# A two-layer graph network: the score stage with its products reordered, background work handed out per product, and VectorE in program order

## The chip, the cores and the metric

The kernel runs on one core of a Trainium2 chip. The core has a matrix engine (TensorE, PE in the profile; its weight loads are PEld), three engines for elementwise work (VectorE or DVE, ScalarE or ACT, GpSimd or POOL) and a queue that issues loads (SyncE, SP). PE writes only to PSUM, which has eight banks here; the others work between PSUM and SBUF, and DMA engines carry data between SBUF and the main memory (DRAM). The metric is the device time in microseconds (us).

## The reference

N = 2708 nodes, 1024 features, two layers, all in float32. `adj` is a 2708 x 2708 matrix of zeros and ones.

```python
def _L0_gnn_ref(x, adj, Wf, bf, Wg, bg, W, bW):
    f = x @ Wf + bf
    g = x @ Wg + bg
    e = jax.nn.relu(f @ g.T)
    scores = jnp.where(adj > 0, e, NEG)
    attention = jax.nn.softmax(scores, axis=1)
    return attention @ (x @ W + bW)

def _L1_gnn_ref(input, adj, W, a1, a2):
    h = input @ W
    e = jax.nn.leaky_relu(h @ a1 + (h @ a2).T, negative_slope=ALPHA)
    scores = jnp.where(adj > 0, e, neg)
    return jax.nn.relu(jax.nn.softmax(scores, axis=1) @ h)

h = jnp.maximum(_layernorm(x, axis=-1), 0.0)
x = x + _L0_gnn_ref(h, adj, ...)
h = jnp.maximum(_layernorm(x, axis=-1), 0.0)
x = x + _L1_gnn_ref(h, adj, ...)
```

## The kernel before

Every large matrix product is done as seven products of half the size (M1 to M7, the Strassen-Winograd scheme): both operands are split into quarters, sums of quarters are formed, the products are added up in PSUM and by VectorE.

The 2708 nodes are cut into five panels of columns (`panels`): two of 586 and three of 512. Each panel is cut into tiles of 128 rows, the last of a wide panel has 74; two tiles make a pair, and there are eleven pairs (`NQ` = 11). Layer 0 works on scores turned round: for a panel p, `scores(p, B)` (line 823) makes, for each pair q of rows, a block of 256 rows by the panel's columns. Its left sides are the normalized rows h, transposed, as seven sums of quarters; they were stored in DRAM as `hs_d[q]` in the order `BY_SCORES` and are loaded from there two at a time (`As`). Its right sides `B` come from `project_q(p)`, which multiplies h of the panel by the product of the weights.

Within a pair the seven products run in the order M1, M6, M5, M7, M2, M4, M3. X, Y and Z are three PSUM banks: M1 and M2 go to X, M5 and M3 to Y, M6, M7 and M4 to Z. After each product VectorE adds the bank to a tile: `sm1` (`sm` in the profile, two adds) from X, `st` from Z and from Y, then `Sb`, `Sa`, `Sb`, `Sa`. M7 adds to what M6 left in Z, so it may start only when VectorE has read Z; likewise M4 after M7, M3 after M5 and M2 after M1. All these adds go through the helper `add` (line 195); `sub` is line 198. Then the mask is added (line 880), the running maximum `acc` of a column is raised (line 885), and for rows that are `known` the maximum `mx` that layer 1 needs (`raise_max`, line 815).

Between these, `convert(q + 1)` makes the next pair's mask from `adj` on VectorE (lines 533 and 536), and `turn(q + 1)` transposes it on PE (line 546) and copies it on ScalarE (line 547).

Background work is kept in a list `later`, filled by `put(us, go, fetch, takes_psum)`. `behind(us)` adds us to a credit, at most twice us, and runs items while the credit is above zero; `one()` runs the next item and calls the `fetch` (a load) of the next two. `make_until(q)` forces items until the left sides of pair q are made. In the score stage `behind` is called once for a pair, with 4.0 in the first panel and 6.0 in the others. The items in the first panel are those of `make_pairs`: for rows that are not yet ready `norms` (layer norm: statistics on VectorE, a square root and a Relu on ScalarE), `rows` (sums of quarters stored to `hg_d`), `dots`, `transposes` (PE, copied by ScalarE to `hsT`) and `sums` (four VectorE sums, three stores from the GpSimd queue: two to `hs_d` and one of the quarter `a21` to `a21_d`). `hsT` is a pair of tiles with one buffer each, shared with `hT` and `gT`. In later panels the items are those of `rows_done` (line 934): for each finished row tile of layer 0 its layer norm, its two dot products, the sums of its pair and `put_max` for the panels already made.

The order in which each engine meets its instructions is fixed when the kernel is built: a scheduler places them by priority and by its own estimate of when operands are ready. Only the loads (`load`, line 98) are kept in program order on SP. Tiles come from pools: 54 slots, 12 stream buffers (`As`, `adj_i`, the sums `g`), and the eight banks.

Of the kernel before, what the change touches and what calls it, by code (L numbers as in the profile page):

```python
# [29 lines left out]
BY_SCORES = (M1, M6, M5, M7, M2, M4, M3)  # L30
# [3 lines left out]
def kernel(  # L34
# [19 lines left out]
    nc = tc.nc  # L54
# [53 lines left out]
    hs_d = [dram.tile([P, 7, NH, P], FP, name=f"hs_d{q}") for q in range(NQ)]  # L108
    a21_d = [dram.tile([P, NH, P], FP, name=f"a21_d{q}") for q in range(NQ)]
# [94 lines left out]
    def normalize(t):  # L204
# [8 lines left out]
        nc.scalar.activation(rs[:n, :1], mv[:n, 1:2], AF.Sqrt, bias=eps[:n])  # L213
        nc.vector.reciprocal(rs[:n, :1], rs[:n, :1])
# [27 lines left out]
    def make_pairs():  # L242
# [17 lines left out]
        def transposes(q):  # L260
            n = rows_of[q]
            lo, hi = (t[:, :4 * W].rearrange("p (m c j) -> p m c j", m=4, j=P) for t in both("hsT"))
            a21 = slot("a21", (P, NH, P))
            hT[q] = lo, hi, a21
            for k, e, o in ((0, 0, lo[:, 0]), (0, 1, hi[:, 0]), (1, 0, a21), (1, 1, hi[:, 1])):
                ps = bank("h_ps", (P, NH, P))
                for c in range(NH):
                    nc.tensor.transpose(ps[:, c, :n], xs[q][k][e][:, c * P:(c + 1) * P], ident[:n, :n])
                nc.scalar.copy(o[:, :, :n], ps[:, :, :n])

        def sums(q):
            n = rows_of[q]
            lo, hi, a21 = hT.pop(q)
            i = lambda t, k: t[:, k, :, :n]
            b = a21[:, :, :n]
            add(i(lo, 2), b, i(hi, 1))
            sub(i(lo, 1), i(lo, 2), i(lo, 0))
            sub(i(lo, 3), i(lo, 0), b)
            sub(i(hi, 2), i(hi, 0), i(lo, 1))
            if n == P:  # L280
                flat = lambda t, k: t[:, :k].rearrange("p m c j -> p (m c j)")
                nc.gpsimd.dma_start(hs_d[q][:, 0:4].rearrange("p m c j -> p (m c j)"), flat(lo, 4))
                nc.gpsimd.dma_start(hs_d[q][:, 4:7].rearrange("p m c j -> p (m c j)"), flat(hi, 3))
            else:
                nc.gpsimd.dma_start(hs_d[q][:, 0:4, :, :n].rearrange("p m c j -> p (m c) j"),
                                    lo[:, :, :, :n].rearrange("p m c j -> p (m c) j"))
                nc.gpsimd.dma_start(hs_d[q][:, 4:7, :, :n].rearrange("p m c j -> p (m c) j"),
                                    hi[:, :3, :, :n].rearrange("p m c j -> p (m c) j"))
            nc.gpsimd.dma_start(a21_d[q][:, :, :n], b)
# [145 lines left out]
    def project_q(p, then={}):  # L435
# [6 lines left out]
        for t, (_, n) in enumerate(panels[p], first[p]):  # L442
            q, k = pair_of[t]
            load(lo[:, :, o:o + n], hs_d[q][:, 0, :, :n] if k == 0 else a21_d[q][:, :, :n])
# [378 lines left out]
    def scores(p, B):  # L823
# [8 lines left out]
        S = [None] * NT  # L832
        for q in range(NQ):
# [6 lines left out]
            A = {}  # L840

            def product(m, ps, start):
                i = BY_SCORES.index(m)
                if i % 2 == 0:
                    A[i // 2] = stream("As", (P, 2, NH, P))
                    k = min(2, 7 - i)
                    if n == P:
                        load(A[i // 2][:, :k].rearrange("p m c j -> p (m c j)"),
                                          hs_d[q][:, i:i + k].rearrange("p m c j -> p (m c j)"))
                    else:  # L850
                        load(A[i // 2][:, :k, :, :n].rearrange("p m c j -> p (m c) j"),
                                          hs_d[q][:, i:i + k, :, :n].rearrange("p m c j -> p (m c) j"))
                for c in range(NH):
                    nc.tensor.matmul(ps[:n, :h], A[i // 2][:, i % 2, c, :n], B[m][c // 2][:, c % 2, :h],  # L854
                                     start=(start and c == 0), stop=(c == NH - 1), skip_group_check=True)

            X, Y, Z = (bank(f"s{k}") for k in "xyz")
            m1, t = slot("sm1"), slot("st")
            product(M1, X, True)
            for s in (lo, hi):  # L860
                add(m1[:n, s], X[:n, :h], rb[:n, s])
            product(M6, Z, True)
            add(t[:n, lo], Z[:n, :h], m1[:n, hi])
            product(M5, Y, True)
# [3 lines left out]
            product(M7, Z, False)  # L868
            add(sb[:n, hi], Z[:n, :h], t[:n, hi])
            product(M2, X, False)  # L870
            add(sa[:n, lo], X[:n, :h], rb[:n, lo])
            product(M4, Z, False)
            add(sb[:n, lo], Z[:n, :h], m1[:n, lo])
            product(M3, Y, False)
            add(sa[:n, hi], Y[:n, :h], t[:n, lo])
            if q + 1 < NQ:
                turn(q + 1)
            mk = mk_sb.pop((p, q))
            for k, s in enumerate((sa, sb)):
                nc.vector.scalar_tensor_tensor(s[:n, :w], s[:n, :w], 0.0, mk[:n, k, :w], op0=OP.max, op1=OP.add)  # L880
            for k, s in enumerate((sa, sb)):
                if q == 0 and k == 0:
                    nc.vector.tensor_copy(acc[:, :w], s[:, :w])
                else:
                    nc.vector.tensor_tensor(acc[:n, :w], acc[:n, :w], s[:n, :w], OP.max)
            if q in known:
                for k in range(2):
                    raise_max(p, q, k, mk[:n, k, :w])
            behind(4.0 if p == 0 else 6.0, True)
# [44 lines left out]
    def rows_done(t, xt):  # L934
# [4 lines left out]
        def dots():  # L939
            for k in range(2):  # L940
                dot(f[k][:n, t:t + 1], xt, [b[:n] for b in halves(wab[k])])
# [189 lines left out]
```

## Time and profile before

| | |
|---|---|
| times of three runs | 3283.95, 3287.55, 3278.29 us, median 3283.95 |
| the profiled execution | 3277.73 us, span 3276.0 us, mean granted TensorE clock 0.983 |
| HBM | read 535.23 MB, written 113.58 MB |
| `As<-hs_d` loads | 150 of 512 KB and 50 of 256 KB for whole pairs |
| stores of `hsT` to `hs_d` | 10 of 1024 KB (median 9.0 us to landing), 10 of 768 KB (10.5 us) |
| stores to `a21_d` | 10 of 256 KB (7.0 us) |

A line of instruction groups reads: line, engine, operation, output<-inputs by the program's names, shapes, how many | busy time in us, mean ns of one | idle time of the engine just before them, and what ended it. A line of the timeline reads: start, duration (both in us), engine, line, operation, tiles, how many in a row, and in brackets how long the engine had been idle before and what released it. A line of windows gives, for a stretch of the span, its length and each engine's busy time with the number of instructions, then the granted PE clock, the share in which the DMA engines were busy and GB/s. Matmuls of PE overlap: a product of eight matmuls listed at 1.89 or 2.14 us is followed by the next one 1.73 or 1.98 us after its start.

### The profile page before, as it was taken

To read this page: it belongs to the slowest core of one execution; us is meant where nothing else is said; L and a number is where in the kernel's file an instruction comes from. 1 tells how busy PE (TensorE), PEld (TensorE's weight loads), DVE (VectorE), ACT (ScalarE), POOL (GpSimd) and SP (SyncE) were. 2 spreads that over 40 slices of the span, in tenths; PEclk is the share of its full clock that TensorE was granted. 3 is DMA by queue.
4 is the path that set the end of the run, shared out by engine and by line. 5 is a ranking of instruction groups with operands and counts; after the bars stand their busy time and mean duration, and the time that the engine had idled before them with its cause. 6 is when DMAs were issued, how large, how long until landed. Compare 5 with 4: busy or idle time off the path is not lost.

```text
span 3276.0 us, 35270 instructions
## 1 busy us (share of the span) xinstructions
PE 3138.0 (96%) x12924; PEld 2331.6 (71%) x12924; DVE 1743.3 (53%) x3645; ACT 499.8 (15%) x833; POOL 331.4 (10%) x421
## 2 busy tenths in 40 slices
PE   8797899989999999999999999996999999999999
PEld 5375677747877478885788886873766748778585
DVE  6756577165551585616663257637665182553712
ACT  2312120010110110201020002103222030221300
POOL 1411102210001210012000101121010010000001
PEclk9998999999999999999999999998999999999999
DMA  5976848556645487456765566766555445565646
GB/s 216 361 249 246 295 150 323 172 184 209 188 136 156 133 265 222 143 185 196 232 194 149 155 205 208 237 210 238 172 170 174 149 144 182 180 194 176 195 149 212
DMA packets 284829, 651.17 MB, mean 199 GB/s; under 512 B 51919, under 2 KB 121539, under 8 KB 283377
## 3 DMA queue, kind: packets, MB, share of 16 engines
q1 hardware_dynamic: 252480, 535.31, 52.3%
q0 software_dynamic: 32176, 113.62, 9.0%
q8 instruction: 102, 1.67, 0.2%
q14 instruction: 71, 0.57, 0.0%
HBM read 535.23 MB, written 113.58 MB: 198 GB/s over the span
## 4 chain that ended last, share of the span: by engine, by line
PE 42%; issue 4%; DVE 4%; ACT 1%; DMA 0%; POOL 0%; SPq 0%; POOLq 0%; DVEq 0%; ACTq 0%
PE gz L416 8%; PE gy L416 8%; PE gx L416 8%; PE sz L854 3%; PE gv L416 3%; PE pz L752 3%; PE sx L854 2%; PE sy L854 2%; PE px L752 2%; PE py L752 2%; DVE sm L195 1%; DVE P L1053 1%; PE qz L416 1%; DVE P L195 1%; PE qy L416 0%
## 5 line engine op out<-in xcount | busy, mean ns | idle before, releaser
L854 PE MATMUL sz<-B,As 128*128 128x256 f32 (+3 forms) x1320 | 340.4, 402 | 43.9 <-DVE st L195 43.9
L854 PEld LDWEIGHTS sz<-B,As 128*128 128x128 f32 (+1 forms) x1320 | 249.6, 190 | 109.1 <-DVE st L195 49.8
L854 PE MATMUL sx<-B,As 128*128 128x256 f32 (+3 forms) x880 | 225.2, 398 | 9.9 <-DMA As<-hs_d 9.2
L854 PE MATMUL sy<-B,As 128*128 128x256 f32 (+3 forms) x880 | 218.9, 391 | 0.0
L416 PE MATMUL gy<-T,hc 128*128 128x256 f32 (+3 forms) x880 | 206.2, 396 | 5.4 <-DMA hc<-hg_d 3.0
L416 PE MATMUL gx<-P,hc 128*128 128x256 f32 (+3 forms) x880 | 204.5, 394 | 6.0 <-ACT P L1055 4.7
L416 PE MATMUL gz<-Sa,hc 128*128 128x256 f32 (+3 forms) x880 | 206.6, 393 | 0.0
L416 PE MATMUL gz<-P,hc 128*128 128x256 f32 (+3 forms) x880 | 206.3, 393 | 0.0
L687 POOL TENSOR_TENSOR gT<-gT,rr 128x2048 f32<-128x2048 f32 (+3 forms) x20 | 68.3, 3434 | 1316.0 <-DVE rr L134 519.8
L416 PEld LDWEIGHTS gx<-P,hc 128*128 128x128 f32 (+1 forms) x880 | 168.1, 191 | 42.5 <-ACT P L1055 5.0
L416 PEld LDWEIGHTS gy<-T,hc 128*128 128x128 f32 (+1 forms) x880 | 168.7, 192 | 41.4 <-DVE junk L172 3.4
L854 PEld LDWEIGHTS sx<-B,As 128*128 128x128 f32 (+1 forms) x880 | 161.2, 188 | 45.4 <-DVE r L173 9.4
L854 PEld LDWEIGHTS sy<-B,As 128*128 128x128 f32 (+1 forms) x880 | 163.0, 185 | 38.0
L416 PEld LDWEIGHTS gz<-Sa,hc 128*128 128x128 f32 (+1 forms) x880 | 165.5, 190 | 31.9
L416 PEld LDWEIGHTS gz<-P,hc 128*128 128x128 f32 (+1 forms) x880 | 165.5, 190 | 31.9
L547 ACT COPY mask<-mk_ps 128x1024 bf16<-128x1024 bf16 (+1 forms) x55 | 55.7, 1013 | 660.3 <-PE mk_ps L546 301.6
L752 PE MATMUL py<-w,ps 128*128 128x512 f32 (+1 forms) x352 | 155.5, 592 | 0.3 <-issue 0.3
L752 PE MATMUL px<-w,gT 128*128 128x512 f32 x320 | 144.8, 605 | 11.0 <-issue 9.6
L752 PE MATMUL pz<-w,ps 128*128 128x512 f32 (+1 forms) x352 | 155.0, 592 | 0.0
L752 PEld LDWEIGHTS pz<-w,ps 128*128 128x128 f32 (+1 forms) x352 | 65.4, 186 | 85.6 <-issue 82.5
L752 PEld LDWEIGHTS py<-w,ps 128*128 128x128 f32 (+1 forms) x352 | 65.4, 186 | 85.6 <-issue 83.2
L752 PEld LDWEIGHTS px<-w,gT 128*128 128x128 f32 x320 | 61.5, 194 | 87.2 <-issue 83.3
(240 smaller groups left out, 4721.9 us busy)
## 6 DMA issues: line engine op xcount, KB each, us to landing
hc<-hg_d SPq DMA_DIRECT2D x350, 512.0 KB
As<-hs_d SPq DMA_DIRECT2D x150, 512.0 KB
w<-wt_d SPq DMA_DIRECT2D x96, 512.0 KB
w<-in_L_gnn_W_dram SPq DMA_DIRECT2D x72, 512.0 KB
md<-md_d SPq DMA_DIRECT2D x70, 512.0 KB
adj_i<-in_adj_dram SPq DMA_DIRECT2D x50, 512.0 KB
hg_d<-g POOLq DMA_DIRECT2D x40, 512.0 KB, 5.9
As<-hs_d SPq DMA_DIRECT2D x50, 256.0 KB
```

Of the source, the lines that this page charges most:

```text
L195: nc.vector.tensor_tensor(o, a, b, OP.add)
L416: nc.tensor.matmul(ps[d], left(m, k, d), right(m, k), start=(start and k == 0), stop=(k == K - 1), skip_group_check=True)
L547: nc.scalar.copy(mk[:n, :, :k4 * P], ps[:n, :, :k4 * P])
L687: nc.gpsimd.tensor_tensor(of(e, s), of(e, s), by(s, k), OP.mult)
L752: nc.tensor.matmul(ps, left[i][m][:, k, :], w_[k], start=(start and k == 0), stop=(k == NH - 1), skip_group_check=True)
L854: nc.tensor.matmul(ps[:n, :h], A[i // 2][:, i % 2, c, :n], B[m][c // 2][:, c % 2, :h], start=(start and c == 0), stop=(c == NH - 1), skip_ ...
L1053: nc.vector.scalar_tensor_tensor(s, ub[:n, :w], f[1][:n, t:t + 1], s, op0=OP.add, op1=OP.max)
```

## The change

The order of products becomes M1, M6, M5, M2, M7, M3, M4, and a pair's M4 is issued after the next pair's M1 (`left_over`, `last`). Background work is handed out after each product: 0.6 in the first panel and 1.0 in the others, twice that after M3. From the first pair to the last of a score stage, every VectorE instruction is pinned behind the one traced before it on that engine (`InOrder`, `hold`). The mask, `acc` and `raise_max` of each half are done as soon as it is ready (`finish`). The layer norm of a row tile is split into `moments` and `normalize`, and the two dot products into two items. The quarter `a21` becomes an eighth block of `hs_d`, and the seven blocks stand there in the new order.

```diff
-BY_SCORES = (M1, M6, M5, M7, M2, M4, M3)
+BY_SCORES = (M1, M6, M5, M2, M7, M3, M4)
+class InOrder:
+    class Engine:
...
+        def __getattr__(self, name):
+            f = getattr(self.engine, name)
+            def issue(*a, **k):
+                i = f(*a, **k)
+                return self.owner.tc.keep_in_program_order(i) if self.owner.hold else i
+            return issue
...
-    nc = tc.nc
+    nc = InOrder(tc)
...
-    hs_d = [dram.tile([P, 7, NH, P], FP, name=f"hs_d{q}") for q in range(NQ)]
-    a21_d = [dram.tile([P, NH, P], FP, name=f"a21_d{q}") for q in range(NQ)]
+    hs_d = [dram.tile([P, 8, NH, P], FP, name=f"hs_d{q}") for q in range(NQ)]
...
         rs = stats.tile([P, 2], FP, name="rs")
         nc.scalar.activation(rs[:n, :1], mv[:n, 1:2], AF.Sqrt, bias=eps[:n])
+        of_rows[id(t)] = mv, rs
+    def normalize(t):
+        n = t[0].shape[0]
+        if id(t) not in of_rows:
+            moments(t)
+        mv, rs = of_rows.pop(id(t))
         nc.vector.reciprocal(rs[:n, :1], rs[:n, :1])
...
-            a21 = slot("a21", (P, NH, P))
-            hT[q] = lo, hi, a21
-            for k, e, o in ((0, 0, lo[:, 0]), (0, 1, hi[:, 0]), (1, 0, a21), (1, 1, hi[:, 1])):
+            hT[q] = lo, hi
+            for k, e, o in ((0, 0, lo[:, 0]), (0, 1, lo[:, 3]), (1, 0, hi[:, 3]), (1, 1, hi[:, 2])):
...
-            add(i(lo, 2), b, i(hi, 1))
+            add(i(lo, 2), i(hi, 3), i(hi, 2))
             sub(i(lo, 1), i(lo, 2), i(lo, 0))
-            sub(i(lo, 3), i(lo, 0), b)
-            sub(i(hi, 2), i(hi, 0), i(lo, 1))
+            sub(i(hi, 0), i(lo, 0), i(hi, 3))
+            sub(i(hi, 1), i(lo, 3), i(lo, 1))
...
-                nc.gpsimd.dma_start(hs_d[q][:, 4:7].rearrange("p m c j -> p (m c j)"), flat(hi, 3))
+                nc.gpsimd.dma_start(flat(hs_d[q][:, 4:8]), flat(hi))
...
-            nc.gpsimd.dma_start(a21_d[q][:, :, :n], b)
...
+        rate = 0.6 if p == 0 else 1.0
+        lefts = {}
...
+        def finish(q, s, k):
+            n, mk = rows_of[q], mk_sb[p, q]
+            nc.vector.scalar_tensor_tensor(s[:n, :w], s[:n, :w], 0.0, mk[:n, k, :w], op0=OP.max, op1=OP.add)
...
+                nc.vector.tensor_tensor(acc[:n, :w], acc[:n, :w], s[:n, :w], OP.max)
+            if q in known:
+                raise_max(p, q, k, mk[:n, k, :w])
+        def last(q, sb, Z, m1):
+            n = rows_of[q]
+            product(q, M4, Z, False)
+            add(sb[:n, lo], Z[:n, :h], m1[:n, lo])
+            finish(q, sb, 1)
+            mk_sb.pop((p, q))
+            behind(rate, True)
+        nc.hold = True
+        left_over = None
         for q in range(NQ):
...
-            product(M1, X, True)
+            product(q, M1, X, True)
             for s in (lo, hi):
                 add(m1[:n, s], X[:n, :h], rb[:n, s])
-            product(M6, Z, True)
+            if left_over:
+                left_over()
+            product(q, M6, Z, True)
             add(t[:n, lo], Z[:n, :h], m1[:n, hi])
-            product(M5, Y, True)
+            behind(rate, True)
+            product(q, M5, Y, True)
             add(t[:n, hi], Y[:n, :h], m1[:n, hi])
             if q + 1 < NQ:
                 convert(q + 1)
-            product(M7, Z, False)
+            behind(rate, True)
+            product(q, M2, X, False)
+            add(sa[:n, lo], X[:n, :h], rb[:n, lo])
+            behind(rate, True)
+            product(q, M7, Z, False)
             add(sb[:n, hi], Z[:n, :h], t[:n, hi])
...
+            behind(rate, True)
             if q + 1 < NQ:
                 turn(q + 1)
...
-            behind(4.0 if p == 0 else 6.0, True)
+            product(q, M3, Y, False)
+            add(sa[:n, hi], Y[:n, :h], t[:n, lo])
+            finish(q, sa, 0)
+            behind(2 * rate, True)
+            left_over = lambda q=q, sb=sb, Z=Z, m1=m1: last(q, sb, Z, m1)
+        left_over()
+        nc.hold = False
...
-        put(2.1, lambda: normalize(xt))
-        put(3.2, dots)
+        put(1.5, lambda: moments(xt))
+        put(0.5, lambda: normalize(xt))
+        put(1.6, lambda: dots(0))
+        put(1.6, lambda: dots(1))
```

## The prediction

> **What bounds the kernel now.** I read the busy times first, then the costliest groups with what ended the idle time before them, then busy times cut into the five score stages, and last the timelines of TensorE (PE), VectorE (DVE), ScalarE and the load queue (SP) around each gap.
>
> ```profile
> PE 3138.0 (96%) x12924; PEld 2331.6 (71%) x12924; DVE 1743.3 (53%) x3645; ACT 499.8 (15%) x833; POOL 331.4 (10%) x421
> ...
> L854 PE MATMUL sz<-B,As 128*128 128x256 f32 (+3 forms) x1320 | 340.4, 402 | 43.9 <-DVE st L195 43.9
> ...
> L854 PE MATMUL sx<-B,As 128*128 128x256 f32 (+3 forms) x880 | 225.2, 398 | 9.9 <-DMA As<-hs_d 9.2
> ```
>
> PE is the bound: only 138 us of the 3276.0 us span are not busy. 53.8 of these (43.9 + 9.9) stand before the score products of L854, which the change touches. Nearly all of them end with VectorE's `st`, one with a load of `As`.
>
> ```profile
> core 0: us, PE busy (x) PEld busy (x) DVE busy (x) ACT busy (x) POOL busy (x), PEclk, DMA share, GB/s
> 225.00:431.40 206.40, 179.95 (x831) 136.46 (x830) 116.59 (x229) 33.20 (x61) 22.98 (x41) 0.93 0.74 252
> 701.50:872.90 171.40, 160.81 (x720) 120.18 (x718) 95.63 (x193) 15.51 (x26) 11.62 (x20) 0.97 0.67 209
> 1149.00:1298.00 149.00, 140.89 (x698) 118.89 (x697) 100.70 (x216) 13.65 (x16) 16.99 (x24) 0.99 0.80 253
> 1530.60:1679.80 149.20, 140.53 (x698) 118.75 (x697) 98.99 (x204) 14.04 (x16) 14.10 (x20) 0.98 0.77 241
> 1864.30:2002.20 137.90, 137.90 (x698) 118.11 (x697) 79.18 (x155) 10.13 (x10) 17.81 (x18) 1.00 0.68 209
> ```
>
> The rows are the score stages P0 to P4, from first product to last. P4 has no gap at full clock: 137.9 is the floor for 256 columns, so P2 and P3 lie 11.1 and 11.3 above it. At 293 columns products start 1.98 apart and a pair's mask transposes take 0.53: 77 x 1.98 + 10 x 0.53 = 157.5, so P1 lies 13.9 above. P0 also holds seven sets of transposes of x at 1.77, floor 169.9: 36.5 above. Together **72.8 us**: 53.8 of idle PE and 19 of half clock after the gaps. That is all the change can win there.
>
> ```profile
> 255.58 4.27 PE L854 MATMUL sz<-B,As 128*128 128x293 f32 x8 [8.29 <-DVE st L195]
> ```
> ```profile
> 1573.02 5.84 DVE L815 SCALAR_TENSOR_TENSOR mx<-maskl,f,mx 128x586 f32<-128x586 bf16 x8
> ```
> ```profile
> 340.25 0.69 DVE L198 TENSOR_TENSOR hsT<-hsT,a 128x512 f32<-128x512 f32 x1 [8.41 <-ACT hsT L269]
> ```
> ```profile
> 339.63 0.59 ACT L269 COPY hsT<-h_ps 128x512 f32<-128x512 f32 x1 [10.46 <-DMA hs_d<-hsT]
> ```
> ```profile
> 267.36 13.86 SPq L98 DMA_DIRECT2D x<-in_x_dram  x4
> 281.31 0.39 SPq L98 DMA_DIRECT2D adj_i<-in_adj_dram  x1
> 281.79 0.31 SPq L98 DMA_DIRECT2D adj_t<-in_adj_dram  x1
> 282.15 1.77 SPq L98 DMA_DIRECT2D As<-hs_d  x4
> ```
>
> Three kinds of gap. First, order: M7 adds to the bank that held M6 and may start only when VectorE has read it, but VectorE had background work ahead of that add (rows, dots and norms of later rows at 241 to 254 and 706 to 715, a run of 5.84 us of `mx` at 1573). Second, a true wait: in P0 VectorE stood 8.41 us because ScalarE could not write `hsT` until the previous pair's store had landed. Third, SP: four loads of x waited for room and held the next pair's `As` back; PE then stood 9.23 us to 291.89.
>
> **The change, part by part.** *Reorder.* Products, matmuls and loads per pair are the same: 7, 56, 4. In before, one product (M5, 1.73 or 1.98 us) stands between M6 and M7, and one (M2) between M7 and M4. In after two stand everywhere (M5, M2; M3 and the next M1; M2, M7), and three between M1 and M2. VectorE may be late by 3.5 us (256 columns) or 4.0 (293) instead of 1.7 or 2.0. M4's `As` load moves behind the next pair's adjacency load and first `As` load on SP; it is needed a product after that first one, so it costs nothing while SP runs ahead. The last `Sb` of a stage comes an add, a max and an `acc` after the last product (0.42 + 2 x 0.69); `acc` is read only after 32 `qx` matmuls (6.9 us), which hide it.
>
> *Program order.* Every VectorE instruction of the stage stands where the code has it. This ends the first kind of gap. Behind a waiting instruction now stand all later adds, and PE waits for them once the 3.5 to 4.0 us are used up.
>
> *Background.* 7 x 0.6 = 4.2 us per pair instead of 4.0 in P0, 7.0 instead of 6.0 later, in pieces. Splitting normalize and dots adds no instruction; the Sqrt (0.29) falls between two handed-out pieces. VectorE's budget: P4 has 10.4 of `mx` in 79.2, so a pair needs (79.2 - 10.4)/11 = 6.3 without it. P2 has 18.4 on `x_res` and about 9 of loaded-mask `mx`: 27.4, spread by 7.0 over 3.9 pairs. In those VectorE has 27.4 + 3.9 x 7.3 (6.3 and about 1 of inline `mx`) = 55.9 against 3.9 x 12.59 = 49.1 of PE: 6.8 over, less 3.5 of grace, 3.3, plus about 2 for waits on ScalarE's Relu (rows of 0.55 to 1.25): **P2 keeps 5** of 11.1 (1 to 11). P3: 12.0 + 9.6 = 21.6 over 3.1 pairs, 44.9 against 39.0, likewise **4** of 11.3 (1 to 11). P1: 15 over 2.1 pairs at 7.4, 30.5 against 30.3: **1** of 13.9 (0 to 8, the start's backlog). P4: 0 (0 to 3). Without the grace P2 and P3 would keep 7 more. The pairs' `hg_d` stores on POOL and mask loads on SP move with the pieces; `hg_d` is read only in the aggregation, over 100 us later.
>
> *P0, by the same reckoning of credit.* (a) The gap of 8.29 and its slow product (4.07 instead of 1.98) go: 0 left. (b) The code still asks for pair 10's four x loads just ahead of pair 3's `As`, into a pool where one slot is freed (`a21`) and one `sm1` and a mask live longer. 9.23 and 2.9 of half clock stay, or go: 0 to 12; no row decides; **6**. (c) Pairs 6 to 10 of `hsT` follow through one buffer. From the last of its four sums to the next pair's last sum: issue 0.8, landing 10.8, copies 1.7, sums 2.8, about 16. The code puts them 8, 10, 12 and 14 us of PE work apart, so each is waited for; before, two such waits cost 6.45 and 2.48 with 3.9 of half clock, 12.8. Four waits of the longest seen, 8.4, less 4.0 grace, plus 2.1 clock each, would be 26; none if the spacing absorbs them. Nearest is before's row: **13**. (d) At pair 4 `rows`, `dots`, and pair 6's sums are forced in one piece: 2.8 + 3.4 + 2.8 = 9.0 ahead of `sm`; M2 comes due at 9.7 and `sm` at about 11.9, so 2.2 and 0.8 of clock: **3** (0 to 6). P0 keeps **22** of 36.5 (0 to 44).
>
> *One store instead of two.* 11 POOL issues of 0.55 us fewer, on an engine 10% busy; the second `hs_d` store grows from 768 to 1024 KB. By the rows of issue to landing (9.0 us for 1024 KB, 10.5 for 768 KB) that is -1.5 to +1.5 where the first projection waits for it; taken as 0.
>
> **Sum.** 72.8 - (22 + 1 + 5 + 4 + 0) = 41 us less. I allow 6 either way for later stages, whose schedule is laid anew, and take 39. The profiled execution took 3277.7 (span 3276.0 and 1.7 around it), which would become 3239; the median of the runs shown is 3283.95, so 3245.
>
> The Trainium skill, Perfetto Trace Analysis, Optimization Strategy, says that bubbles which recur can mean that SBUF or PSUM has no room for the next tile. That speaks against the change, since no reordering makes room. SP's wait on slots agrees at one place; by the rule alone (b) and (c) would stay whole and the sum be 35. TensorE: Matmul & The Clock Gate, What's actually happening, says that the clock halves after an idle window of about 3.4 us. The gap of 2.48 us at 362 was followed by a product of 3.76 instead of 1.98, so this trace shows it for less; by the rule the leftovers in P2 and P3 cost no clock.
>
> **Rivals.** *Only P1 to P3 heal*, P0 keeps 36.5: gain 72.8 - 36.5 - 10 = 26, time **3258**. For it: (b) and (c) are waits for room, not order. Against: the 8.29 gap is order. *Nearly all heals*: 8 left, **3219**. For it: P4 runs without a gap. Against: the 16 us chain. *Cancelled*: (b) 12, (c) 26, (d) 6 and two new waits on `hsT` at 6.5 make P0 57, with 18 kept in P1 to P3 75 against 72.8: **3286**, no change. *Slower*: VectorE's fixed order waits at its head. Place: the seven sums of P0 and the norms and dots of P1 to P3. Price: 7 x (8.4 - 4.0 + 2.1) + 3 + 12 = 60 in P0; 12 tiles at 2.3 (the longest wait of dots for Relu), the overloads 6.8 and 5.9 without grace, and six slow clocks of 2.1, 53, in P1 to P3. 113 against 72.8: **3324**. It decides once the held-up time passes 72.8; with P1 to P3 at 10, each of the seven waits would have to last 8.7. For it: the row of 8.41. Against: before's two sums were asked for back to back, after's are apart. That the order is not kept would be seen as hoisted work; it falls under the middle cases.
>
> **How the numbers follow.** Forecast 0.40, only P1 to P3 0.24, nearly all 0.10, cancelled 0.10, slower 0.16. A difference under 0.3%, 10 us, cannot be told from none. Faster: the first three, less 0.01, 0.73; same 0.10; slower 0.17. The forecast's own range is 3221 to 3266 (leftovers of 10 to 55). For 8 in 10 it goes from 3212 (5 left, and 4 less in later stages) to 3292 (P0 at 44, the others at their upper ends of 8, 11, 11 and 3, and 4 more in later stages).
>
> **What would show it.** VectorE: no background between M1's end and `sm` in P1; `mx` in ones and twos. PE: idle before L854 about 25 instead of 53.8; P1 near 159, P2 and P3 near 142, P0 near 192. Wrong if `hsT` waits grow beyond 8 us, if PE waits for `As` at more pairs, or if P4 leaves 137.9.

## The result, and the profile after

The changed kernel takes 3251.74 us (median of four runs, 3249.0 to 3252.34) beside 3282.73 for the kernel before (four runs): ratio 0.9904, 95% interval 0.9887 to 0.9921, 31 us less. The profiled execution took 3251.27 with a span of 3249.5, 26.5 less than the span of before. The profiled execution of before (3277.73) was quicker than its four timed runs, so the two traces show somewhat less than the medians.

The page's busy times and the score products, with the idle time before them in the last column:

```profile
PE 3136.1 (97%) x12924; PEld 2330.0 (72%) x12924; DVE 1753.1 (54%) x3648; ACT 499.9 (15%) x833; POOL 326.2 (10%) x410
...
L877 PE MATMUL sz<-B,As 128*128 128x256 f32 (+3 forms) x1320 | 327.5, 397 | 2.9 <-DVE st L44 2.9
...
L877 PE MATMUL sx<-B,As 128*128 128x256 f32 (+3 forms) x880 | 224.2, 398 | 13.0 <-DMA As<-hs_d 9.5
```

The 43.9 us in front of `sz` are down to 2.9, and what stands in front of `sx` is the load of `As`, as before. Looked at this way 38 us of PE's 53.8 idle before the score products are gone. But the stages, in busy times by window, do not give up 38:

```profile
221.60:413.00 191.40, 177.87 (x832) 134.78 (x830) 114.45 (x230) 33.80 (x61) 19.55 (x34) 0.96 0.78 271
681.00:845.00 164.00, 160.50 (x720) 120.08 (x718) 97.66 (x199) 15.80 (x27) 12.39 (x22) 0.99 0.68 218
1121.00:1268.50 147.50, 140.52 (x699) 118.80 (x698) 102.94 (x214) 13.76 (x16) 15.29 (x22) 0.99 0.77 252
1501.00:1648.20 147.20, 140.50 (x699) 119.03 (x698) 101.42 (x207) 14.34 (x17) 14.39 (x21) 0.99 0.75 245
1832.60:1975.40 142.80, 139.97 (x699) 119.34 (x698) 86.36 (x156) 10.13 (x10) 18.47 (x19) 0.99 0.62 198
```

| stage | before | after | above its floor | forecast above floor |
|---|---|---|---|---|
| P0 | 206.4 | 191.3 | 21.4 | 22 |
| P1 | 171.4 | 163.9 | 6.4 | 1 |
| P2 | 149.0 | 147.4 | 9.5 | 5 |
| P3 | 149.3 | 147.2 | 9.3 | 4 |
| P4 | 137.9 | 142.7 | 4.8 | 0 |

A stage's floor is the length that the prediction worked out for it without a gap (169.9, 157.5 and three times 137.9). The stages are 21.4 shorter in sum, where 41 were forecast: P0 by 15.1, P1 by 7.5, P2 and P3 by 1.6 and 2.1, and P4 is 4.8 longer. The first begins 3.4 earlier and the stretch between P0 and P1 is 2.1 shorter; the stretches between the later stages have the same length to 0.1 (276.1, 232.5, 184.5), and the tail is 0.4 longer.

**Where the idle time went.** Seen by tile, the mask transposes on PE (line 574) have a line of idle time that before did not have:

```profile
L574 PE MATMUL mk_ps<-identb,nm x440: 217/219/248, 212.6 to 1954.9; 128*128 128x128 bf16 x134, 128*74 128x128 bf16 x13
...
its engine sat idle before it (us, times) until:
  DVE nm L44: 15.2, 8
```

Eight times PE stood before the transposes until VectorE had made the next pair's mask (`nm`): twice in P1, three times each in P2 and P3. One of them, in the timeline of PE and VectorE:

```profile
1138.82 1.89 PE L877 MATMUL sx<-B,As 128*128 128x256 f32 x8
...
1140.32 0.42 DVE L44 TENSOR_TENSOR st<-sz,sm 128x256 f32<-128x256 f32 x1
...
1142.38 0.41 DVE L44 TENSOR_TENSOR st<-sy,sm 128x256 f32<-128x256 f32 x1
1142.71 0.46 DVE L44 TENSOR_SCALAR nm<-adj_i 128x592 bf16<-128x592 int32 x1
...
1143.22 0.64 PE L574 MATMUL mk_ps<-identb,nm 128*74 128x128 bf16 x8 [2.51 <-DVE nm L44]
1143.70 1.95 PE L877 MATMUL sz<-B,As 128*128 128x256 f32 x8
```

M7 (`sz`) was ready at 1140.74, when `st` had been read out of Z. It started at 1143.70, because on PE the transposes stand ahead of it. The code has them behind M7. Only VectorE is pinned: PE's order was still laid by the scheduler, and in these eight pairs it put the transposes between M2 and M7. That its estimate of when the mask is ready led it to do so is argued, not shown.

**P4** lost to something else. Around its one wait:

```profile
1957.29 7.37 POOL L1038 TENSOR_TENSOR x_res<-x_res,bwb 128x512 f32<-128x512 f32 x6
...
1957.49 7.72 DVE L44 SCALAR_TENSOR_TENSOR Sa<-Sa,mask 128x512 f32<-128x512 f32 x1
...
1966.66 0.70 PE L877 MATMUL sx<-B,As 128*128 128x256 f32 x2 [2.83 <-DVE sm L44]
```

One VectorE instruction that takes 0.69 us elsewhere took 7.72, beside six GpSimd adds of 7.37 together. Before, these adds ran from 1992.4, where VectorE had almost only additions that read PSUM, which no GpSimd instruction of these traces does.

**P0** has the waits that the prediction named under (b) and (c), in PE's timeline:

```profile
272.25 4.25 PE L877 MATMUL sx<-B,As 128*128 128x293 f32 x8 [5.64 <-DMA As<-hs_d]
...
294.41 3.34 PE L877 MATMUL sx<-B,As 128*128 128x293 f32 x8 [2.58 <-DMA As<-hs_d]
...
316.39 1.11 PE L299 MATMUL h_ps<-ident,x 128*128 128x128 f32 x4 [2.38 <-DVE Sa L44]
...
331.24 2.25 PE L877 MATMUL sz<-B,As 128*128 128x293 f32 x8 [2.92 <-DVE st L44]
```

### The profile page after: what moved, and what is told of

Same layout as the page of the kernel before. It is cut to its first block, busy times and chain, and to the rows that moved or that the text cites. A ratio compares the mean times of both kernels' runs of the same rounds, so it can differ in the third digit from the quotient of the medians.

```text
span 3249.5 us, 35289 instructions
## 1 busy us (share of the span) xinstructions
PE 3136.1 (97%) x12924; PEld 2330.0 (72%) x12924; DVE 1753.1 (54%) x3648; ACT 499.9 (15%) x833; POOL 326.2 (10%) x410
## 4 chain that ended last, share of the span: by engine, by line
PE 77%; issue 6%; DVE 4%; DMA 3%; POOL 1%; ACT 1%; POOLq 0%; SPq 0%; DVEq 0%; ACTq 0%
PE gz L444 12%; PE gy L444 12%; PE gx L444 12%; PE sz L877 7%; PE sy L877 5%; PE gv L444 5%; PE sx L877 5%; PE pz L780 4%; PE py L780 3%; PE px L780 3%; PE qz L444 3%; PE qy L444 2%; PE qx L444 2%; DMA hs_d<-hsT 1%; PE mk_ps L574 1%
## 5 line engine op out<-in xcount | busy, mean ns | idle before, releaser
L877 PE MATMUL sz<-B,As 128*128 128x256 f32 (+3 forms) x1320 | 327.5, 397 | 2.9 <-DVE st L44 2.9
L780 PE MATMUL px<-w,gT 128*128 128x512 f32 x320 | 145.1, 606 | 11.9 <-issue 10.4
```

Of the source, the lines that this page charges most:

```text
L780: nc.tensor.matmul(ps, left[i][m][:, k, :], w_[k], start=(start and k == 0), stop=(k == NH - 1), skip_group_check=True)
L877: nc.tensor.matmul(ps[:n, :h], lefts[q][:, i % 2, c, :n], B[m][c // 2][:, c % 2, :h], start=(start and c == 0), stop=(c == NH - 1), skip_g ...
```

## The experiments

All are edits of the changed kernel. Times are medians beside runs of the kernel before on the same chip (3280.6 to 3283.5 us); stage lengths are from one trace each.

| kernel | time | ratio to before, 95% | P0 | P1 | P2 | P3 | P4 |
|---|---|---|---|---|---|---|---|
| changed | 3251.7 | 0.9904 (0.9887 to 0.9921) | 191.3 | 163.9 | 147.4 | 147.2 | 142.7 |
| changed, again | 3253.4 | 0.9904 (0.9886 to 0.9921) | 192.9 | 163.9 | 148.0 | 147.2 | 142.7 |
| VectorE's order free | 3251.9 | 0.9901 (0.9888 to 0.9915) | 193.8 | 167.9 | 142.6 | 144.5 | 141.4 |
| background in one lump | 3279.4 | 0.9981 (0.9972 to 0.9990) | 188.2 | 168.5 | 161.8 | 157.6 | 141.4 |
| old order of products | 3279.2 | 0.9984 (0.9975 to 0.9993) | 193.1 | 169.4 | 154.6 | 157.9 | 139.8 |
| transposes later in the code | 3262.0 | 0.9931 (0.9918 to 0.9943) | 194.0 | 163.9 | 146.6 | 149.3 | 146.2 |
| late bias | 3257.4 | 0.9925 (0.9911 to 0.9940) | 193.2 | 163.8 | 147.2 | 149.0 | 137.9 |
| x fetched later | 3247.7 | 0.9901 (0.9885 to 0.9918) | 186.5 | 163.8 | 146.5 | 145.4 | 142.6 |
| 0.75 a product | 3246.0 | 0.9889 (0.9875 to 0.9904) | 190.8 | 162.5 | 140.5 | 149.1 | 142.7 |
| transposes pinned on PE | 3250.0 | 0.9901 (0.9884 to 0.9919) | 193.6 | 158.5 | 149.1 | 145.5 | 145.5 |
| pinned, x later, bias on VectorE | 3240.4 | 0.9872 (0.9856 to 0.9888) | 186.3 | 158.5 | 149.5 | 144.2 | 137.9 |
| the same with 0.75 | 3235.4 | 0.9853 (0.9836 to 0.9869) | 185.7 | 162.3 | 139.2 | 145.5 | 137.9 |
| the same, bias on GpSimd with gaps | 3230.1 | 0.9838 (0.9824 to 0.9853) | 187.0 | 160.6 | 138.5 | 144.9 | 137.9 |

**How far one trace can be trusted.** The changed kernel was run once more:

> The changed kernel once more, unaltered, on the chip of the next two: what two profiles of one kernel differ by. All theories: 3247-3256, stages of P1 to P4 within 1 of 163.9, 147.4, 147.2 and 142.7; P0 and the stretch between P0 and P1, which wait for DMAs, may differ by 2 to 4 us each; VectorE's instruction of 7.7 us in P4 is there again.

P1 to P4 came back within 0.6 us, with the same waits at the same pairs and the long VectorE instruction (7.73). P0 was 1.6 longer, and the stretch between P0 and P1 272.7 against 268.1. The span was 3255.3, 20.7 less than before's. So differences of 2 us in P0 or 5 in a whole span say nothing. In P1 to P4 a difference of 2 us is more than these two traces differ by, though not by much more than happens: the last two kernels of the table have the same code up to P4 and differ by 1.7 in P1.

**What does it: order, pieces or reorder?** Three kernels each take one part away.

```diff
-        nc.hold = True
```

> The changed kernel with VectorE's instructions no longer pinned: products reordered, background still in pieces, the order left to the scheduler. Theory 'order': the gain comes from background no longer standing ahead of the adds that a product waits for; without the pin the scheduler hoists it again, PE's idle time before the score products rises from 13 to 30 us or more and the time from 3252 to 3262-3277. Rival 'slack': the reorder alone gives VectorE two products of room, which covers whatever order the scheduler lays; then the time stays at 3248-3256 and the score stages at their lengths (191, 164, 147, 147, 143).

3251.9, the same time as with the pin: my theory that the pinned order brings the gain falls. The idle time before the score products shows what the pin gives and takes:

```profile
L877 PE MATMUL sz<-B,As 128*128 128x256 f32 (+3 forms) x1320 | 323.0, 393 | 8.5 <-DVE st L44 7.2
...
L877 PE MATMUL sx<-B,As 128*128 128x256 f32 (+3 forms) x880 | 224.1, 398 | 21.1 <-DVE sm L44 14.8
L877 PE MATMUL sy<-B,As 128*128 128x256 f32 (+3 forms) x880 | 223.9, 397 | 4.2 <-DVE st L44 4.2
```

Without the pin PE idles 8.5 + 21.1 + 4.2 = 33.8 us before the score products: background ran ahead of `sm` at the start of P1 (a wait of 6.80) and ahead of `st` in P0 (3.80 and 6.88). With it PE idles 2.9 + 13.0 there, 15.2 before the mask transposes and 2.4 before transposes of x, 33.5 (without it 0.5 before the two kinds of transposes). The pin ends one kind of wait and makes another of the same size.

```diff
-            behind(rate, True)
...
-            behind(2 * rate, True)
+            behind(7 * rate, True)
```

The five single calls go, the one behind M3 hands out all.

> The changed kernel with the same background credit (4.2 us a pair in the first stage, 7.0 later) handed out once, after M3, instead of in seven pieces; VectorE still in program order. Theory 'pieces matter': a lump of 7 us is 3.5 us more than the room that two products give, so about 3.5 us and a slow product of 2 are lost for each of the some 4 + 4 + 3 pairs with a full lump in the second to fourth stage, and a few in the first: 3275-3300. Rival 'room alone': the lump stands where Sa is done and the next M1 needs nothing, so that three products cover it: 3250-3258.

3279.4, as the theory had it. PE idles 47.5 us before `sx`, nearly all for `sm`, the first add behind the lump:

```profile
L877 PE MATMUL sx<-B,As 128*128 128x256 f32 (+3 forms) x880 | 235.8, 413 | 47.5 <-DVE sm L44 42.4
```

P2 and P3 are 14.4 and 10.4 longer than in the changed kernel and longer than before. P0, where a lump is 4.2 us, is not (188.2). The lump of 7.0 is also more than the 6.0 of the kernel before; the new order with 6.0 in one lump was not run.

```diff
-            product(q, M2, X, False)
-            add(sa[:n, lo], X[:n, :h], rb[:n, lo])
-            behind(rate, True)
             product(q, M7, Z, False)
             add(sb[:n, hi], Z[:n, :h], t[:n, hi])
             behind(rate, True)
+            product(q, M2, X, False)
+            add(sa[:n, lo], X[:n, :h], rb[:n, lo])
+            behind(rate, True)
             if q + 1 < NQ:
                 turn(q + 1)
+            last(q, sb, Z, m1)
             product(q, M3, Y, False)
...
-            left_over = lambda q=q, sb=sb, Z=Z, m1=m1: last(q, sb, Z, m1)
-        left_over()
```

> The changed kernel with the products in the order of before (M1, M6, M5, M7, M2, M4, M3, no product left over for the next pair); pieces of background after each product, VectorE in program order, one store of a pair's sums as in the changed kernel. Theory 'both are needed': VectorE may be late by one product (1.7 or 2.0 us) instead of two, and pieces of 1 to 2.7 us beside the two adds after M1 exceed that several times a stage: PE idle before the score products 25 to 45 us, time 3265-3290. Rival 'order of VectorE is enough': 3250-3258.

3279.2, again as the theory had it: in the old order the same pieces cost P2 7.2 and P3 10.7 us more, though of P2's idle time 3.97 us end with a load of masks and not with VectorE. So with one of the two parts taken away 4 us of the 31 are left in the whole time. In P2 and P3 two products of room are about as much as one piece needs and not enough for a lump; one product is not enough for a piece.

By stage this explains less than it seems. P0 fell from 206.4 to 191.3 and stays at 188.2 to 193.8 in all three kernels, so neither the pin, nor the pieces, nor the reorder is needed for the largest part of the gain by itself. What the three share besides (the sums stored with `a21` in two stores instead of three, a tile less, the mask added half by half, 4.2 us of background instead of 4.0) was not taken away, so the cause in P0 stays open. P1, 7.5 shorter, gives back 4.0 to 5.5 without any one of the three. P2 and P3 gained only 1.6 and 2.1; without the pieces or without the reorder both stages are longer than before, with 7.0 us of background a pair instead of 6.0.

**The wait before the mask transposes.** First the transposes were moved in the code alone:

```diff
-            if q + 1 < NQ:
-                turn(q + 1)
             product(q, M3, Y, False)
+            if q + 1 < NQ:
+                turn(q + 1)
```

> The changed kernel with the next pair's mask transposes placed behind M3 instead of ahead of it; nothing else. Theory 'new wait': what P1 to P3 kept (6 to 9 us each) is PE standing in order before these transposes until VectorE has made the next mask (3.5, 5.7 and 6.1 us by the trace); one product more of room ends most of it: P1 to P3 shorter by 10 to 15 us together, time 3237-3244. Rival 'overload': VectorE has more work than PE in those pairs and the wait only moves to sx, sy or sz: stages shorter by less than 3, time 3249-3254.

3262.0, slower than either theory said, and the eight waits are there at the same pairs (14.7 us instead of 15.2). One of them:

```profile
1146.53 1.89 PE L877 MATMUL sx<-B,As 128*128 128x256 f32 x8
1150.42 0.64 PE L574 MATMUL mk_ps<-identb,nm 128*74 128x128 bf16 x8 [2.00 <-DVE nm L44]
1150.90 1.95 PE L877 MATMUL sz<-B,As 128*128 128x256 f32 x8
```

The transposes still follow M2 and precede M7: in 32 of the 40 pairs of P1 to P4 they moved behind M3, in these eight the scheduler put them where it had before. So this run does not decide between the theories. Of the 10 us that it is slower P4 has 3.5 (a wait of 4.94 instead of 2.83 at the long instruction, which lasts 8.51 here). The rest is spread over P0, P3 and the stretch between P0 and P1; in P0 and that stretch it is about what the second trace of the changed kernel has too, and in P3 it is a wait for `sm` that is looked at below. The next kernel pins them:

```diff
-                    nc.tensor.transpose(ps[:n, k, i * P:(i + 1) * P], m[0][:, i, k, :n], identb)
+                    o = nc.tensor.transpose(ps[:n, k, i * P:(i + 1) * P], m[0][:, i, k, :n], identb)
+                    if nc.hold:
+                        tc.keep_in_program_order(o)
```

> The changed kernel with the mask transposes behind M3 in the code and each of them pinned behind the instruction traced before it on PE, so that they stand there on the chip too (in the changed kernel and with the transposes merely moved in the code, 8 of the 40 pairs of P1 to P4 have them ahead of M7, 2, 3 and 3 in P1, P2 and P3, as many as there are waits for nm). Theory 'PE's order': M7 was ready while PE stood before the transposes; the waits for nm fall from 15.3 to under 4 us, P1 to 159-162, P2 and P3 to 140-143, time 3237-3245. Rival 'overload': VectorE is behind by as much in sum, PE then waits before sz or sy for st, or before sx for sm; P1 to P3 shorter by less than 4 together, 3248-3255.

The waits for `nm` are gone, all 15.2 us. P1 fell by 5.4 to 158.5, one above its floor: there the theory holds. P2 rose by 1.7, P3 fell by 1.7, as the rival said: PE now waits for `st` (2.23 in P2, 0.49 to 0.77 in P3), for `sm` (1.97 at the start of P3) and, in P2, 4.00 us for `As`. P4 is 2.8 longer, where M7 takes a wait of 4.93 for the long instruction. The three stages together are 5.4 shorter, between what the theory and the rival said, and the time is the same within the interval. The stand before the transposes was a place, not the whole cause; the work that made VectorE late stayed.

**How much background a pair can take.**

```diff
-        rate = 0.6 if p == 0 else 1.0
+        rate = 0.6 if p == 0 else 0.75
```

> The changed kernel with 0.75 instead of 1.0 us of background after each product in the second to fifth stage, 5.25 instead of 7.0 a pair. Theory 'overload': with the 7.3 us that a pair needs of VectorE itself, 7.0 make 14.3 against 12.6 of PE, and the excess of some four pairs is what P2 and P3 kept; 5.25 make 12.55, so the waits before the mask transposes (5.7 and 6.1) go, P2 and P3 fall from 147 to 139-143, P1 by 0-5, time 3237-3244. Rival 'where a piece stands': pieces are as large as before (2.7, 1.5, 1.6 us) and still stand ahead of the next mask, in more pairs; P2 and P3 stay at 145 or more, time 3248-3254.

P2 fell to 140.5 as the theory said, 2.6 above its floor. P3 did not fall (149.1): its waits for `nm` are shorter, 3.8 us instead of 6.1, but PE waited 3.64 us for `sm` at the start. The time, 3246.0, lies between the two forecasts and is not told apart from the changed kernel's. The same wait stands in the last-but-one kernel of the table, where it is the only one left in P3:

```profile
1495.37 0.81 ACT L249 ACTIVATE x_res<-x_res,rs 128x512 f32<-128x512 f32 x1 [4.08 <-DMA x_d<-x_res]
1496.22 0.69 DVE L44 SCALAR_TENSOR_TENSOR junk<-x_res,wab 128x512 bf16<-128x512 f32 x1 [4.92 <-ACT x_res L249]
...
1497.77 0.74 DVE L44 TENSOR_TENSOR sm<-sx,rb 128x256 f32<-128x256 f32 x2
1498.57 1.65 PE L879 MATMUL sx<-B,As 128*128 128x256 f32 x3 [4.52 <-DVE sm L44]
```

ScalarE's Relu writes over `x_res` in place and waits until its store has landed; the dot product waits for the Relu; `sm` stands behind the dot product on VectorE; M2, which adds to X, waits for `sm`. This is the mechanism of the rival called *Slower*, a wait at VectorE's head, at one place. The wait for `sm` at the start of P3 is 0.6 us in both traces of the changed kernel and 0.6 to 4.5 in the others that have it; where it is longest (2.8 to 4.5), ScalarE waited 2.5 to 4.1 for that store. Handing the Relu another tile was not tried.

**P4.** First the adds were moved out of the stage:

```diff
-                    nc.gpsimd.tensor_add(xs[t][e], xs[t][e], bwb[e][:n, :W])
+                    if p != NP - 2:
+                        nc.gpsimd.tensor_add(xs[t][e], xs[t][e], bwb[e][:n, :W])
...
             add(xs[t][e], c, xs[t][e])
+            if p == NP - 2:
+                nc.gpsimd.tensor_add(xs[t][e], xs[t][e], bwb[e][:n, :W])
```

> The changed kernel with GpSimd's eight adds of the bias bwb to the residual rows of the fourth panel moved from where the rows are loaded (inside the last score stage) to behind VectorE's add in the projection that follows. Theory 'GpSimd holds VectorE up': the instruction Sa<-Sa,mask of 7.72 us lay beside six of these adds (7.37 us together); without them it takes 0.69, the wait of 2.83 us before sx and the slow product go, the fifth stage falls from 142.7 to 137.9-138.5 and the time by 4-5 us to 3246-3249. Rival 'something else held it' (the loads of these rows, or the mask): an instruction of VectorE beside the row loads is long again, the stage stays at 141 or more, time 3250-3254.

P4 is 137.9, its floor, without a wait: GpSimd's adds had held VectorE up. The time did not follow (3257.4): in the projection behind it PE waited 6.35 us for `pt` from VectorE instead of 2.72, and one of the moved adds took 4.06. The stretch behind the stage is 1276.4 us, against 1274.1 and 1272.5 in the two traces of the changed kernel, so 2.3 to 3.9 of the 4.8 went back there; why the median is higher still is not explained. The last kernel of all (otherwise the one with 0.75 under *Together*) leaves the adds in the stage but puts something between them that reads nothing:

```diff
-                    nc.gpsimd.tensor_add(xs[t][e], xs[t][e], bwb[e][:n, :W])
+                    i = nc.gpsimd.tensor_add(xs[t][e], xs[t][e], bwb[e][:n, :W])
+                    if p == NP - 2:
+                        tc.keep_in_program_order(i)
+                        for _ in range(4):
+                            tc.keep_in_program_order(nc.gpsimd.memset(gap, 0.0))
```

> The last one, but with the fourth panel's bias left on GpSimd and four small memsets (128 x 8) between one add and the next. It asks how VectorE came to stand for 7.7 us beside six adds of 1.2 us. Theory 'held add by add': GpSimd takes the shared way into SBUF again before VectorE can, back to back; with something between that reads no SBUF, VectorE's instruction gets in after one add, takes 0.7 to 2.5 us, and P4 is 137.9-139. Rival 'held as long as adds are queued, whatever lies between' or 'memsets hold it too': an instruction of 7 us or more, P4 142-147. The rest as in the run before, within 3 us.

```profile
1952.90 1.26 POOL L1041 TENSOR_TENSOR x_res<-x_res,bwb 128x512 f32<-128x512 f32 x1
1952.96 1.75 DVE L44 TENSOR_TENSOR acc<-acc,Sa 128x512 f32<-128x512 f32 x1
1954.10 0.59 POOL L1045 MEMSET gap<- 128x8 f32 x4
1954.63 0.41 DVE L44 TENSOR_TENSOR Sb<-sz,sm 128x256 f32<-128x256 f32 x1
1954.68 1.26 POOL L1041 TENSOR_TENSOR x_res<-x_res,bwb 128x512 f32<-128x512 f32 x1
1955.08 1.41 DVE L44 SCALAR_TENSOR_TENSOR Sb<-Sb,mask 128x512 f32<-128x512 f32 x1
```

VectorE's instructions with both operands in SBUF now wait for one add at most (1.75 and 1.41 instead of 0.69), the one that reads PSUM takes its usual 0.41, and P4 is at its floor. That is what the theory said. The adds are spread by the memsets too, so that fewer meet VectorE; both belong to the edit. And the memsets are not the only way in: in the kernel with the old order of products GpSimd's first four adds follow each other with nothing between, and VectorE takes turns with them.

```profile
1989.79 6.33 POOL L1039 TENSOR_TENSOR x_res<-x_res,bwb 128x512 f32<-128x512 f32 x4
1990.00 1.63 DVE L44 SCALAR_TENSOR_TENSOR Sb<-Sb,mask 128x512 f32<-128x512 f32 x1
1991.66 1.65 DVE L44 TENSOR_TENSOR acc<-acc,Sb 128x512 f32<-128x512 f32 x1
...
1993.68 1.32 DVE L44 SCALAR_TENSOR_TENSOR Sa<-Sa,mask 128x512 f32<-128x512 f32 x1
```

So adds back to back can hold VectorE for all of them, and need not. What decides is open.

**P0.**

```diff
-    EARLY, AHEAD = 4, 5
+    EARLY, AHEAD = 4, 4
```

> The changed kernel with rows of x fetched four pairs ahead of their sums instead of five (AHEAD 4): in the first stage the loads of pair 10's rows come one pair of sums later, four slots fewer are held, and pair 8's, 9's and 10's norms stand between more of the sums. Theory 'slots hold SP': the two waits for As (5.64 and 2.58 us) and their slow products (2.3 and 1.4) come from loads that stand on SP for a slot; they go or fall below 3 together, and the sums of pairs 4 to 7 are further apart; first stage from 191.3 to 180-186, time 3241-3247. Rival 'room is short whichever way': the wait for a slot only moves to another load of the stage, As is late by the same sum at another pair; stage 189-195, time 3249-3256.

The first stage is 186.5, and 185.7 to 187.0 in the three later kernels that have this edit, against 190.8 to 194.0 in the six traces with five pairs ahead and the pin and pieces of the change. One of the two waits for `As` went, the other grew to 4.50, and waits for `hsT` appeared (2.10, 0.53). In the changed kernel SP stood 15.8 us before the first of the four loads of x, until an `Sb` of VectorE was done that gave a slot free, with `As` behind. So the slots do hold SP at the first wait. At the second it stood 19.8 us before a load of `adj_t`, until VectorE had read an earlier one (`nmt`), and that wait stayed. The edit holds four slots fewer and also moves the loads of x to a later place; no run tells the two apart. The time of this kernel alone is not told apart from the changed one.

**Together.** The parts that paid in their stages were joined: transposes pinned behind M3, AHEAD 4, and the fourth panel's bias on VectorE.

> The last one (transposes behind M3, pinned on PE) together with AHEAD 4 and with the bias of the fourth panel's rows added by VectorE instead of GpSimd. Three stages answer three questions. P1 to P3 as in the run before. P0: 184-188 as with AHEAD 4 alone (186.5), if the parts don't touch. P4: 137.9-139 if it was GpSimd's adds that held VectorE up, since eight adds of 0.69 us are 5.5 us on an engine with 4 us idle a pair; rival: VectorE waits at its head for a load of these rows, P4 141-146. Time 3229-3239 if all three hold, 3240-3248 if PE's order does not pay.

3240.4, at the lower end of what was forecast if PE's order does not pay. All five stages are as expected, P2 and P3 near those of the kernel before. (VectorE's eight adds of the bias run behind P4, from 1963.9 on, so P4 shows what it is without GpSimd's and without VectorE's.) P2 is still 11.6 above its floor. The timeline of PE and SP shows the wait for `As` that was 4.00 with the transposes pinned:

```profile
1152.54 3.13 SPq L121 DMA_DIRECT2D maskl<-mk_d  x4
...
1155.78 4.49 SPq L121 DMA_DIRECT2D adj_i<-in_adj_dram  x1
...
1160.71 3.16 SPq L121 DMA_DIRECT2D As<-hs_d  x4
...
1165.59 5.39 SPq L121 DMA_DIRECT2D As<-hs_d  x4
...
1170.64 1.65 PE L879 MATMUL sx<-B,As 128*128 128x256 f32 x3 [4.44 <-DMA As<-hs_d]
```

The background asks for its mask loads as it is handed out, and SP takes them in order, ahead of `As`. The longest single stand of SP there is within the load of `adj_i`: it waits 4.0 us until VectorE has done with an `mx`, so VectorE's lateness is in it as well. The next kernel therefore takes the lower rate as well:

> The last kernel (transposes behind M3 and pinned on PE, AHEAD 4, the fourth panel's bias on VectorE) with 0.75 instead of 1.0 us of background after each product of the later stages. In P2 a wait for As of 4.4 us had taken the place of the waits for nm: the pair's background, done early, let eight mask loads and an adjacency load stand on SP ahead of As. Theory 'SP is behind because pieces come too fast': with fewer pieces a pair P2 falls from 149.5 to 139-142, P3 from 144.2 to 140-144, P1 158-159, P4 138; time 3228-3236. Rival 'room': As waits as long at another pair, P2 146 or more, time 3237-3243.

3235.4, with P2 at 139.2, both as the theory had it. P1 and P3 are not: P1 is 3.8 longer than at the full rate and P3 1.3, both with one wait for `sm` at the start (2.13 and 4.52). With the bias back on GpSimd between memsets the time is 3230.1, 21.6 below the changed kernel and 53 below the kernel before: the lowest median of all. Its gain over 3235.4 is not explained by P4, which is the same; the stretch behind the stage is 2.8 shorter, where VectorE has eight adds fewer. The other 3.5 us between the two traces lie ahead of P4, where the two kernels have the same code.

## Why the prediction was right, and where it was not

The direction and the size of the whole came out: 3245 forecast, 3251.7 measured, 31 us less instead of 39. That it came so near is in part luck. By its steps it was less good, since the stages gave 21.4 (19.4 in the second trace) of the 41 forecast, and the medians differ by more than the stages for reasons that no run settles: runs of one kernel differ by several us in stretches that the change does not touch.

*P0: 22 forecast, 21.4 and 23.0 measured, in other parts.* (a) went to zero as forecast. (b) was put at 6 of 0 to 12 and cost 13.0: 5.64 and 2.58 idle, and 4.8 in the slow products behind them, read from start to start. (c) was put at 13 and cost 6.8: 2.38 and 2.92 idle and 1.5 of slow clock. VectorE waited 6.05, 3.69, 1.34 and 1.79 us for `hsT` there, not four times 8.4. (d), 3, shows no gap. That the errors cancel is luck. The page's rule weighed in the prediction, that a recurring bubble can mean no room for the next tile (the Trainium skill, Perfetto Trace Analysis, Optimization Strategy), fits (b): the new order left waits for `As`, and holding four slots fewer, with the loads later, ended one of two.

*P1 to P3: 10 forecast, 25.1 measured.* This is the term that was mis-sized, and the step behind it is the grace. The prediction gave VectorE 3.5 us of lateness in which PE finds other products, because two products stand between a read and its reuse. But PE also has transposes of the next mask, in a fixed place, and these wait for VectorE too. The prediction asked what stands behind a waiting instruction on VectorE and not what on PE waits for `convert`. PE's idle time before the score products fell to 15.9, lower than the 25 forecast, and 15.2 stood before the mask transposes instead. The prediction weighed that what is left in P2 and P3 might cost no clock; each of the two has one stretch of 3.41 us at half clock, behind waits of 2.23 and 3.42. "Without the grace P2 and P3 would keep 7 more" (twice 3.5) was too little: the kernel in the old order, which has half of the grace, keeps 7.2 and 10.7 more. P3's sum is also added up wrongly (21.6 and 3.1 pairs at 7.3 make 44.2, not 44.9), which leaves its 4 as it is. The budget itself (7.0 of background and 7.3 of a pair's own work against 12.59) was sound for P2, which falls to 2.6 above its floor at 5.25, and not the limit in P3.

*P4: 0 to 3 forecast, 4.8 measured.* The one stage without a gap was taken as safe. GpSimd's adds start 18 us before the stage's end (1957.3 of 1975.4) where they started 10 before it (1992.4 of 2002.2), as the loads of their rows do (the first 25 us before the end instead of 20), and met VectorE's mask addition. This and the waits for `As` (at three pairs of P0 and P2 instead of one) are two of the prediction's three signs of being wrong; the third, waits for `hsT` beyond 8 us, did not come.

*Program order.* "This ends the first kind of gap" was right as to that gap, which comes back without the pin, and wrong as to its worth: the pin pays 0 in sum, since with it PE waits elsewhere. The whole gain of 31 needs the reorder and the pieces together, but most of P0's 15.1 us are there when either one is missing, and why is open.

*Of the rivals*, *Only P1 to P3 heal* is refuted, and nearly turned round: P0 fell by 15.1 and P1 to P3 by 11.2 of the 26 it counted. The mechanism of *Slower* was found alive at one place, the Relu that waits for a store, at 0.6 us in the changed kernel.

## What to carry to other kernels

Room in the order of products and work in pieces can be worth little alone and much together: compare the largest piece with the time between a result and its reuse, and look at every stage for itself, since here the largest gain, in P0, needs neither of the two by itself. If one engine is pinned to program order, look where the scheduler puts the other engines' instructions that wait for it: pinning VectorE alone left eight sets of transposes waiting 15.2 us, against 0.2 without the pin. A transfer that comes earlier brings its consumer earlier too, and may set it against an engine that was alone there.

## What the hardware showed

VectorE's addition of the mask, both operands in SBUF, took 7.71 to 7.73 us in six traces beside six GpSimd adds of some 1.26 each, 8.49 and 8.51 in two beside eight, and 0.69 alone. The Trainium skill, SBUF — State Buffer, Who interferes with whom, says that a VectorE instruction with two SBUF inputs contends with a GpSimd instruction that reads SBUF, and not with one that only writes it, and calls what they share an exclusive lock. The traces agree, with one thing more: adds issued back to back kept VectorE out until the last of them, with memsets between them for one (1.75), but in one trace back-to-back adds let VectorE in after each (1.32 to 1.65).

PE's clock does not follow from the length of a gap alone: in the changed kernel a gap of 2.92 us was followed by a product of 2.25, nearly the usual 2.14, and one of 2.58 by a product of 3.34. The granted clock in the traces changes only in steps of 3.41 us from a fixed start. In busy times by window, with the granted clock behind them, the steps in which the two gaps end, and the steps that follow:

```profile
291.95:295.36 3.41, 0.95 (x4) 0.80 (x5) 3.36 (x7) 0.71 (x2) 1.05 (x2) 1.00 1.01 377
295.36:298.77 3.41, 3.41 (x9) 2.35 (x8) 3.25 (x10) 0.00 (x0) 0.40 (x1) 0.50 1.04 412
...
329.49:332.91 3.42, 1.67 (x7) 1.33 (x8) 3.24 (x8) 0.00 (x0) 1.47 (x2) 1.00 0.93 356
332.91:336.32 3.41, 3.41 (x32) 3.12 (x31) 0.47 (x1) 0.00 (x0) 0.00 (x0) 1.00 0.97 342
```

The gap of 2.58 lies with 2.46 in one step, and the next step has half clock. The one of 2.92 is cut into 1.17 and 1.75, and the clock stays whole. In all fourteen traces, the ends of the span left out, every step at full clock in which PE idled for more than 2.02 us was followed by half clock, and every one with less than 1.8 us by full clock, with one exception (1.50).
